# Layer 0's last four token tiles put among the first products of layer 1's convolution

## The chip, the cores and the metric

The kernel runs on one core of one Trainium2 chip. The metric is the device time of one execution in microseconds (us), the median of several runs. Engines are named as in the profile: PE is TensorE, DVE is VectorE, ACT is ScalarE, POOL is GpSimd, and SP issues nearly all DMAs. TensorE's loads of weights are shown as PEld.

## What is computed

Four transformer-like layers follow one another, each with an attention part and a feed-forward part, and each part ends in `x = layernorm(x + part(x))`. x has two samples of 1024 tokens and 1024 channels here. The change lies between the feed-forward part of layer 0 and the attention part of layer 1:

```python
# layer 0, feed-forward: a block-diagonal MLP on permuted channels
t = x[:, perm].reshape(tokens, 16, 64)
t = gelu(t @ up) @ down                  # per block, 64 -> 256 -> 64
x = layernorm(x + t.reshape(tokens, 1024)[:, argsort(perm)])
# layer 1, attention: first a convolution of width 3 along the tokens
y = conv1d(x, conv_w, "SAME") + conv_b   # 1024 -> 768 channels: q, k, v
# then attention in blocks of 128 tokens, 16 heads, and a projection
```

## The kernel before

The two samples are computed one after the other. Of a sample, `x` holds the eight tiles of 128 tokens (tokens on the partitions), and `xT` the same values turned (channels on the partitions, eight blocks k of 128 channels), with one zero column at either end for the convolution. Halves of 512 tokens are called th=0 (tiles 0 to 3) and th=1 (tiles 4 to 7).

**The end of layer 0** (`l0`). `blocks(th, extra)` runs the eight pairs of MLP blocks of one half: `ups` and `downs` on PE (L391, L409), `gelus` on ACT (L399), and a copy to `o` on DVE (L417) that POOL scatters by rows to `yd[th]` in DRAM by an indirect DMA (L418), which undoes the permutation. Each scatter waits for the one before it, since both write `yd[th]`. `back(th)` loads `yd[th]` again as eight pieces `y` of 128 channels by 512 tokens (L436, SP). For each tile `add_y` turns eight pieces of 128x128 on PE (L443) into two PSUM tiles, adds them to `x` on DVE (L131) and takes the statistics of the norm (`ln_stats`, L142 and L143); `ln_roots` makes the reciprocal roots (L150, ACT L156 and L157, DVE L159 to L162), `ln_scale` the norm itself (L165), and `to_xT` turns the tile on PE (L120) and copies it to `xT`, half on DVE (L97) and half on ACT (L99). The four tiles of th=0 are done inside `blocks(1)`. Those of th=1 come after it, tiles 4 and 5 with common roots, then tiles 6 and 7.

**The start of layer 1** (`l1_attn`). A pool opens with parameters and buffers (`qkv`, `qh`, `kh`, `u0`); it takes the place of `l0`'s pools, so its first writers wait until those are free. The convolution of width 3 makes two tokens at a time: four sums or differences of shifted columns of `xT` (j = 0 to 3), each multiplied by a weight of its own. For th=0 DVE writes these sums into `qh` (j = 0, 1) and `kh` (j = 2, 3), 256 columns for each of eight channel blocks (L546, eight operations of 128x1024); they see tokens -1 to 511 for j = 0, 1, 2, and to token 512 for j = 3. For th=1 POOL writes them in place into `xT` and `u0` (L546, 32 operations of 128x256). `conv(th, co)` is one of the six blocks of 128 output channels: it loads weights, multiplies 4 x 8 times (L579; each call shows as two matmuls of 256 columns in the trace, and j = 0, 1 share one PSUM tile, j = 2, 3 another), and puts the four together (`ce` on ACT L585, `cf` on DVE L589, `qkv` on DVE L592). This text calls the six blocks of th=0 c0 to c5. In sample 0 the two combined weights are made on DVE (L566 to L568, 128x1024 each) and stored to `cvd` in DRAM (L570), from where sample 1 and the second half load them.

In sample 0 c0 to c3 are followed by one step of `l2_dequant` each, which prepares a weight of layer 2: loads of scales and packed values (L1371, L1373), on DVE two unpackings (L1378, L1380) and two scalings (L1381), and two scatters to `wq` by POOL (L1382). All these weights share the pool `wp` with eight buffers of 512 KB, so a load waits until the last reader of a buffer is done. SP issues its DMAs in one order, and a DMA that waits holds all behind it.

**Who sets the order.** Inside `with self.tc.manual_schedule():` each engine gets its instructions in the order in which they are written. Outside, a scheduler orders them by priority when the program is built. Before, `l0`'s block is written by hand up to the norms of tiles 4 and 5; the tail with tiles 6 and 7 and the whole convolution of th=0 are left to the scheduler. What follows (heads, attention, the convolution of th=1) is by hand again and is not touched.

Of the kernel before, what the change touches and what calls it, by code (L numbers as in the profile page):

```python
# [8 lines left out]
F = mybir.dt.float32  # L9
# [8 lines left out]
P = 128  # L18
B = 2
S = 1024  # L20
D = 1024
NT = S // P
KD = D // P
HALF = 512
# [3 lines left out]
class Net:  # L28
# [96 lines left out]

    def add_row(self, row, tt):
        self.nc.gpsimd.tensor_tensor(self.x[:, tt, :], self.x[:, tt, :], row, ALU.add)

    def add_x(self, tt, half, p):
        xs = self.x[:, tt, half * HALF : (half + 1) * HALF]  # L130
# [62 lines left out]
    def l0(self, b):  # L193
        nc, i = self.nc, self.i
# [8 lines left out]
        with self.tc.tile_pool(name=self.nm("l0a"), bufs=1) as lp, self.tc.tile_pool(name=self.nm("l0b"), bufs=2) as tp:  # L203
# [27 lines left out]
            for th in range(2):  # L231
                for s, dst in ((0, qT), (1, kT), (2, v)):
                    p = self.ps()
# [202 lines left out]
                    nc.sync.dma_start(t, yd[th][k * P : (k + 1) * P, :])  # L436
                return ys

            def add_y(tt, ys):
                for g in range(2):  # L440
                    p = self.ps()
                    for j in range(4):
                        nc.tensor.transpose(  # L443
                            p[:, j * P : (j + 1) * P], ys[4 * g + j][:, (tt % 4) * P : (tt % 4 + 1) * P], self.ident
                        )
                    self.add_x(tt, g, p)
                self.ln_stats(tt)

            def line(th, first, n):


# [13 lines left out]
            with self.tc.manual_schedule():  # L465
                self.table()
                maxima(0)
                attend(0, {})
                maxima(1)
                e = line(0, project, (0, 1, 3, 4, 5, 6, 7, 8, 9))  # L470
                at(e, 9, lambda: store(0))
                at(e, 9, lambda: gather(0))
                attend(1, e)
                project(4)
                project(5)
                e = line(1, project, (-1, -1, 0, 0, 1, 1, 2, 2, 3))
# [7 lines left out]
                e = line(0, lambda tt: add_y(tt, ys), (2, 3, 3, 4, 5, 6, 6, 7, 7))  # L484
                blocks(1, e)
                ys = back(1)
                self.table()
                add_y(4, ys)
                add_y(5, ys)
                self.ln_roots([4, 5])  # L490
                for tt in (4, 5):
                    add_y(tt + 2, ys)
                    self.ln_scale(tt)
                    self.to_xT(tt)

        self.ln_roots([6, 7])
        for tt in (6, 7):
            self.ln_scale(tt)
            self.to_xT(tt)

    def l1_attn(self, b):
        nc, i = self.nc, self.i
        row = self.row("l1_projb")
        with self.tc.tile_pool(name=self.nm("l1a"), bufs=1) as lp, self.tc.tile_pool(name=self.nm("l1s"), bufs=2) as spool:
# [13 lines left out]
            nc.gpsimd.tensor_copy(identr, self.ident)  # L522
            bv = self.row("l1_bv")
            qkv = lp.tile([P, 6, S], F, name=self.nm("qkv"))

            qh = lp.tile([P, 8, HALF], F, name=self.nm("qh"))
            kh = lp.tile([P, 8, HALF], F, name=self.nm("kh"))
            u0 = lp.tile([P, HALF], F, name=self.nm("u0"))
# [29 lines left out]
            def conv(th, co):  # L558

                w = {}  # L560

                def load():
                    g = [self.w(i["l1_conv"][co, 0])]
                    if b == 0 and th == 0:
                        g1, g2, t = self.w(i["l1_conv"][co, 1]), self.w(i["l1_conv"][co, 2]), self.w()
                        nc.vector.tensor_tensor(t, g[0], g2, ALU.add)  # L566
                        nc.vector.tensor_tensor(t, t, g1, ALU.add)
                        nc.vector.scalar_tensor_tensor(g1, g1, -2.0, t, ALU.mult, ALU.add)  # L568
                        for n, f in enumerate((t, g1)):
                            nc.sync.dma_start(self.cvd[co, n], f)  # L570
                        w["w"] = [t, g1, g[0], g2]
                    else:
                        es = [self.w(self.cvd[co, n]) for n in range(2)]
                        w["w"] = es + g + [self.w(i["l1_conv"][co, 2])]

                def call(j, k):
                    if k == 0 and j % 2 == 0:
                        w["p", j // 2] = self.ps()
                    nc.tensor.matmul(  # L579
                        w["p", j // 2][:, 256 * (j % 2) : 256 * (j % 2) + 256], w["w"][j][:, k * P : (k + 1) * P],  # L580
                        moving(th, j, k), start=k == 0, stop=k == KD - 1,
                    )
                    if (j, k) == (2, 1):
                        w["e"] = spool.tile([P, 256], F, tag="ce", bufs=1, name=self.nm("ce"))
                        nc.scalar.activation(w["e"], w["p", 0][:, :256], AF.Identity, bias=cb2[:, co : co + 1])  # L585
                    if (j, k) == (2, 4):
                        w["f"] = spool.tile([P, HALF], F, tag="cf", bufs=1, name=self.nm("cf"))
                        for n, op in enumerate((ALU.add, ALU.subtract)):
                            nc.vector.tensor_tensor(w["f"][:, 256 * n : 256 * n + 256], w["e"], w["p", 0][:, 256:], op)  # L589

                def last():
                    nc.vector.scalar_tensor_tensor(  # L592
                        qkv[:, co, th * HALF : (th + 1) * HALF].rearrange("p (i s) -> p s i", s=2),
                        w["f"].rearrange("p (s i) -> p s i", s=2), 0.5,
                        w["p", 1].rearrange("p (s i) -> p s i", s=2), ALU.mult, ALU.add,
                    )

                return load, [lambda j=j, k=k: call(j, k) for j in range(4) for k in range(KD)], last

            first = conv(0, 0)  # L600
            first[0]()
            for j in range(4):
# [1196 lines left out]
```

## Time and profile before

| | us |
|---|---|
| median of 3 runs (5542.56 to 5547.45) | 5543.17 |
| the profiled execution, its own time | 5559.85 |
| its span in the profile | 5557.9 |
| PE busy in it | 5115.4 |
| DVE busy | 3199.0 |
| ACT busy | 1936.1 |
| POOL busy | 2021.7 |

The profile is of one execution, on the one core that is used; the granted TensorE clock was 0.948 of full speed over the span. Times in the prediction's steps are positions in this span. Sample 0 passes from layer 0 to layer 1 near 371 to 413 us, sample 1 near 3149 to 3185 us. In a line of the timeline the columns are start, duration, engine, line, operation, output and inputs, shapes and count; in brackets the idle time before it and what ended it. In a table by stage each engine's busy time stands in the order PE, PEld, DVE, ACT, POOL with its count of instructions.

### The profile page before, as it was taken

The numbers are of one execution on the slowest core, as the hardware profiler recorded it, in microseconds if no ns is written. First come the engines' busy times: TensorE is split into PE (matmuls) and PEld (weight loads), VectorE is DVE, ScalarE is ACT, GpSimd is POOL, SyncE is SP. The second block draws the span as 40 slices with busy tenths as digits, with TensorE's granted clock in tenths as the row PEclk, the third lists the DMA queues.
The fourth block names the chain that finished last, engine by engine and source line by source line (L and its number), as shares of the span: only waits on it lengthen the run. The fifth ranks groups of instructions, "written<-read, shape, count | busy, mean of one in ns | idle before, by whom it ended". The sixth has DMA issues, their size and how long they took to land.

```text
span 5557.9 us, 52406 instructions
## 1 busy us (share of the span) xinstructions
PE 5115.4 (92%) x17864; PEld 2586.7 (47%) x17864; DVE 3199.0 (58%) x4410; ACT 1936.1 (35%) x3925; POOL 2021.7 (36%) x1195
## 2 busy tenths in 40 slices
PE   9869989999999999998989799799999999999989
PEld 4436746444444444453444376464444444444533
DVE  3553245249999997214345412452599899953243
ACT  2230222257766542001013312222677665410110
POOL 1021220057778884100010211200677788831010
PEclk8789998999999999999988899989999999999999
DMA  2035310267787996110110333012777889951100
GB/s 92 33 131 174 103 43 33 100 182 221 210 234 222 259 258 197 61 60 13 55 63 33 115 123 103 32 44 87 212 215 204 243 219 264 264 177 45 61 8 30
DMA packets 263134, 725.28 MB, mean 130 GB/s; under 512 B 37425, under 2 KB 54449, under 8 KB 262869
## 3 DMA queue, kind: packets, MB, share of 16 engines
q1 hardware_dynamic: 256596, 700.97, 42.4%
q0 software_dynamic: 6272, 20.98, 1.1%
q8 instruction: 142, 2.33, 0.2%
q14 instruction: 124, 1.01, 0.1%
HBM read 616.70 MB, written 103.02 MB: 129 GB/s over the span
## 4 chain that ended last, share of the span: by engine, by line
PE 70%; DVE 14%; DMA 4%; ACT 3%; issue 2%; POOL 1%; SPq 0%; DVEq 0%; POOLq 0%; ACTq 0%
PE ps L104 28%; PE ps L1232 7%; PE ps L1122 6%; PE ps L579 5%; DVE h L1129 4%; PE ps L1151 4%; PE ps L1445 4%; PE ps L1271 3%; DVE h L1140 2%; PE ps L120 2%; PE ps L1185 2%; ACT ps L1124 1%; DVE x L165 1%; DVE st L142 1%; DMA w<-xcd 1%
## 5 line engine op out<-in xcount | busy, mean ns | idle before, releaser
L1114 POOL TENSOR_TENSOR h<-h,br 128x1024 f32<-128x1024 f32 x512 | 1204.3, 2374 | 27.6 <-DMA h<-dxd 20.0
L1124 ACT ACTIVATE ps<-ps,l_Alog 128x512 f32<-128x512 f32 x1024 | 668.8, 660 | 686.0 <-PE ps L1122 671.5
L1122 PE MATMUL ps<-hi,rep 128*128 128x512 f32 x1024 | 758.8, 741 | 22.9 <-DVE h L1129 14.6
L1129 DVE TENSOR_TENSOR_SCAN h<-ps,h 128x512 f32<-128x512 f32 x512 | 606.4, 1213 | 159.9 <-ACT ps L1124 159.8
L1129 DVE TENSOR_TENSOR_SCAN h<-ps,hst,h 128x512 f32<-128x512 f32 x512 | 643.8, 1304 | 11.7 <-ACT ps L1124 11.7
L1140 DVE TENSOR_TENSOR h<-h,ps 128x1024 f32<-128x1024 f32 x512 | 621.4, 1214 | 0.0
L104 PE MATMUL ps<-w,xT 128*128 128x512 f32 (+1 forms) x1280 | 518.3, 562 | 0.0
L1232 PE MATMUL ps<-xT,w 128*128 128x512 f32 x1024 | 511.0, 602 | 0.0
L1151 PE MATMUL ps<-h,sel 128*32 128x512 f32 x2048 | 404.5, 611 | 72.6 <-DVE h L1140 72.3
L1431 POOL TENSOR_TENSOR x<-x,row 128x1024 f32<-128x1024 f32 x48 | 112.9, 2353 | 883.4 <-PE ps L120 883.4
L131 DVE TENSOR_TENSOR x<-x,ps 128x512 f32<-128x512 f32 x192 | 129.9, 687 | 522.9 <-PE ps L104 372.5
L104 PE MATMUL ps<-xT,w 128*128 128x512 f32 x960 | 425.3, 599 | 0.2 <-DMA w<-l_wqkv 0.2
L1122 PE MATMUL ps<-lo,rep 128*128 128x512 f32 x1024 | 408.5, 399 | 0.0
L104 PEld LDWEIGHTS ps<-w,xT 128*128 128x128 f32 x1280 | 247.4, 195 | 255.3 <-issue 248.1
L1122 PEld LDWEIGHTS ps<-hi,rep 128*128 128x128 f32 x1024 | 196.0, 191 | 346.4 <-issue 242.1
L120 PE MATMUL ps<-ident,x 128*128 128x128 f32 x1024 | 168.5, 322 | 182.5 <-DVE x L165 155.8
L156 ACT ACTIVATE rs<-mv 128x1 f32<-128x1 f32 (+2 forms) x94 | 19.1, 203 | 786.4 <-DVE mv L150 786.2
L104 PEld LDWEIGHTS ps<-xT,w 128*128 128x128 f32 x960 | 183.8, 192 | 233.7 <-issue 230.4
L1122 PEld LDWEIGHTS ps<-lo,rep 128*128 128x128 f32 x1024 | 196.7, 192 | 201.0 <-issue 196.4
L1080 POOL TENSOR_TENSOR e<-e,one 128x512 f32<-128x512 f32 x64 | 81.5, 1273 | 563.5 <-ACT one L1077 381.0
L1271 PE MATMUL ps<-w,w 128*128 128x512 f32 x512 | 269.3, 608 | 0.0
L1185 PE MATMUL ps<-xT,w 128*128 128x512 f32 x512 | 266.1, 605 | 2.0 <-DVE h L1129 2.0
(268 smaller groups left out, 7579.6 us busy)
## 6 DMA issues: line engine op xcount, KB each, us to landing
h<-dxd SPq DMA_DIRECT2D x512, 512.0 KB
w<-l_in SPq DMA_DIRECT2D x128, 512.0 KB
w<-l_out SPq DMA_DIRECT2D x96, 512.0 KB
w<-l_conv SPq DMA_DIRECT2D x54, 512.0 KB
w<-cvd SPq DMA_DIRECT2D x36, 512.0 KB
w<-l_fw SPq DMA_DIRECT2D x32, 512.0 KB
xcd<-xo SPq DMA_DIRECT2D x64, 256.0 KB
szd<-zo SPq DMA_DIRECT2D x64, 256.0 KB
```

The source lines that it names most:

```text
L104: self.nc.tensor.matmul(out, lhsT, rhs, start=j == 0, stop=j == n - 1)
L120: nc.tensor.transpose(p[:, j * P : (j + 1) * P], self.x[:, tt, k * P : (k + 1) * P], self.ident)
L579: nc.tensor.matmul(w["p", j // 2][:, 256 * (j % 2) : 256 * (j % 2) + 256], w["w"][j][:, k * P : (k + 1) * P], moving(th, j, k), start=k == ...
L1114: nc.gpsimd.tensor_tensor(hs[k], hs[k], norms[of(k)[0]][1].unsqueeze(1).to_broadcast([P, 2, HALF]), ALU.mult)
L1122: nc.tensor.matmul(dA[k, m], rep[:, 8 * jj + 4 * m + q, :], hl[u, c][n], start=n == 0, stop=n == 1)
L1124: nc.scalar.activation(dA[k, m], dA[k, m], AF.Exp, scale=A[:, g : g + 1])
L1129: nc.vector.tensor_tensor_scan(hs[k][:, m, :], dA.pop((k, m)), hs[k][:, m, :], hst[:, g : g + 1] if u else 0.0, ALU.mult, ALU.add)
L1140: nc.vector.tensor_tensor(hs[k], hs[k], norms[of(k)[0]][3].unsqueeze(1).to_broadcast([P, 2, HALF]), ALU.mult)
L1151: nc.tensor.matmul(py[u, c][32 * j : 32 * j + 32, :], self.sel[:, q, :], hs[k - 1 + j // 2][:, j % 2, :], start=False, stop=q == 3,)
L1185: nc.tensor.matmul(p, w["w"][:, k * P : (k + 1) * P], self.xcols(k, u0, HALF), start=k == 0, stop=k == KD - 1)
L1232: nc.tensor.matmul(p, w["w"][:, k * P : (k + 1) * P], self.xcols(k, u * HALF, HALF), start=k == 0, stop=k == KD - 1)
L1271: nc.tensor.matmul(p, y[:, cc, t * P : (t + 1) * P], wt[:, cc * HALF : (cc + 1) * HALF], start=c2 == 0 and cc == 0, stop=last,)
```

## The change

`add_y` becomes a method of the class with the same body. `l0` ends with `blocks(1, e)` and returns `yd[1]`; the loads of `y` for th=1, and the additions, norms and transposes of tiles 4 to 7, move into `l1_attn`. There the pieces `y` are loaded into `vh`, a buffer of the heads that is empty at that time and is now made with the others. A block in written order holds c0 and c1 by j (eight calls each) with the four tiles between them: c0's j = 0, 1, 2 and c1's j = 0 come before tile 4, c0's j = 3 after tile 4 is turned. c1's `cf` is put into `u0`, so that c0's and c1's are alive together. The weights of c1 and then the pieces `y` are asked for before the first products. POOL's sums for th=1 are written after this block, and `l2_dequant(0)` to `(3)` follow c2 to c5 instead of c0 to c3. In the built order of each engine the instructions of everything after the heads stand as before.

```diff
@@ l0
-                ys = back(1)
-                self.table()
-                add_y(4, ys)
-                add_y(5, ys)
-                self.ln_roots([4, 5])
-                for tt in (4, 5):
-                    add_y(tt + 2, ys)
-                    self.ln_scale(tt)
-                    self.to_xT(tt)
-
-        self.ln_roots([6, 7])
-        for tt in (6, 7):
-            self.ln_scale(tt)
-            self.to_xT(tt)
+        return yd[1]
@@ l1_attn
+            vh = lp.tile([P, 4, D], F, name=self.nm("vh"))
...
                     if (j, k) == (2, 4):
-                        w["f"] = spool.tile([P, HALF], F, tag="cf", bufs=1, name=self.nm("cf"))
+                        if (th, co) == (0, 1):
+                            w["f"] = u0
+                        else:
+                            w["f"] = spool.tile([P, HALF], F, tag="cf", bufs=1, name=self.nm("cf"))
...
-            first = conv(0, 0)
-            first[0]()
-            for j in range(4):
+            def sums0(j):
                 for g in range(2):
                     ks = slice(4 * g, 4 * g + 4)
                     sums(nc.vector, 0, ks, [(j, (qh, kh)[j // 2][:, ks, 256 * (j % 2) : 256 * (j % 2) + 256])])
+            c0, c1 = conv(0, 0), conv(0, 1)
+            with self.tc.manual_schedule():
+                c0[0]()
+                sums0(0)
+                sums0(1)
+                c1[0]()
+                ys = [t for q in range(4) for t in (vh[:, q, :HALF], vh[:, q, HALF:])]
+                for k, t in enumerate(ys):
+                    nc.sync.dma_start(t, yd[k * P : (k + 1) * P, :])
+
+                def calls(c, j):
+                    for f in c[1][8 * j : 8 * j + 8]:
+                        f()
+
+                calls(c0, 0)
+                sums0(2)
+                calls(c0, 1)
+                calls(c0, 2)
+                calls(c1, 0)
+                self.table()
+                self.add_y(4, ys)
+                self.add_y(5, ys)
+                self.ln_roots([4, 5])
+                self.ln_scale(4)
+                self.add_y(6, ys)
+                self.to_xT(4)
+                self.ln_scale(5)
+                sums0(3)
+                calls(c1, 1)
+                self.to_xT(5)
+                calls(c0, 3)
+                c0[2]()
+                c2 = conv(0, 2)
+                c2[0]()
+                self.add_y(7, ys)
+                self.ln_roots([6, 7])
+                calls(c1, 2)
+                self.ln_scale(6)
+                self.to_xT(6)
+                self.ln_scale(7)
+                calls(c1, 3)
+                self.to_xT(7)
+                c1[2]()
             for k in range(KD):
                 sums(nc.gpsimd, 1, slice(k, k + 1), [(j, moving(1, j, k).unsqueeze(1)) for j in (2, 3, 0, 1)])
-            for co in range(6):
-                load, calls, last = conv(0, co) if co else first
-                if co:
+            for co in range(2, 6):
+                load, cs, last = conv(0, co) if co > 2 else c2
+                if co > 2:
                     load()
-                for f in calls:
+                for f in cs:
                     f()
                 last()
-                if b == 0 and co < 4:
-                    self.l2_dequant(co)
-
-            vh = lp.tile([P, 4, D], F, name=self.nm("vh"))
+                if b == 0:
+                    self.l2_dequant(co - 2)
@@ net_kernel
-            net.l0(b)
-            net.l1_attn(b)
+            net.l1_attn(b, net.l0(b))
```

More of the change, by code (lines that the diff above doesn't have):

```diff
@@ L127, in add_row, with add_y @@
         self.nc.gpsimd.tensor_tensor(self.x[:, tt, :], self.x[:, tt, :], row, ALU.add)
+    def add_y(self, tt, ys):
+        for g in range(2):
+            p = self.ps()
+            for j in range(4):
+                self.nc.tensor.transpose(
+                    p[:, j * P : (j + 1) * P], ys[4 * g + j][:, (tt % 4) * P : (tt % 4 + 1) * P], self.ident
+                )
+            self.add_x(tt, g, p)
+        self.ln_stats(tt)
     def add_x(self, tt, half, p):
@@ L437, in back @@
                 return ys
-            def add_y(tt, ys):
-                for g in range(2):
-                    p = self.ps()
-                    for j in range(4):
[L443 to L447, printed above, removed]
             def line(th, first, n):
@@ L483, in l0, with l1_attn @@
                 ys = back(0)
-                e = line(0, lambda tt: add_y(tt, ys), (2, 3, 3, 4, 5, 6, 6, 7, 7))
+                e = line(0, lambda tt: self.add_y(tt, ys), (2, 3, 3, 4, 5, 6, 6, 7, 7))
                 blocks(1, e)
-                ys = back(1)
-                self.table()
-                add_y(4, ys)
-                add_y(5, ys)
-                self.ln_roots([4, 5])
-                for tt in (4, 5):
-                    add_y(tt + 2, ys)
-                    self.ln_scale(tt)
-                    self.to_xT(tt)
-        self.ln_roots([6, 7])
-        for tt in (6, 7):
-            self.ln_scale(tt)
-            self.to_xT(tt)
-    def l1_attn(self, b):
+        return yd[1]
+    def l1_attn(self, b, yd):
         nc, i = self.nc, self.i
@@ L598, in conv @@
                 return load, [lambda j=j, k=k: call(j, k) for j in range(4) for k in range(KD)], last
-            first = conv(0, 0)
-            first[0]()
-            for j in range(4):
+            def sums0(j):
                 for g in range(2):
```

## The prediction

> **What bounds the kernel now.** I read the page first: TensorE (PE) is busy 92% of the span and holds 70% of the chain that ended last, so a change pays where PE stands still. Line 1 and the first line of part 4 of the page:
>
> ```profile
> PE 5115.4 (92%) x17864; PEld 2586.7 (47%) x17864; DVE 3199.0 (58%) x4410; ACT 1936.1 (35%) x3925; POOL 2021.7 (36%) x1195
> PE 70%; DVE 14%; DMA 4%; ACT 3%; issue 2%; POOL 1%; SPq 0%; DVEq 0%; POOLq 0%; ACTq 0%
> ```
>
> Then the table by stage: sample 0 from the last transposes of L0's blocks to the first product of the convolution, its first two output blocks (c0, c1), the pause before c2, c2 to c5; then sample 1: the same without a pause. Columns: stretch, length, busy us of each engine with counts, granted PE clock, DMA share, GB/s.
>
> ```profile
> 371.60:412.90 41.30, 15.59 (x65) 12.78 (x66) 28.27 (x49) 4.44 (x9) 1.29 (x4) 0.63 0.31 106
> 412.90:440.70 27.80, 27.78 (x130) 24.12 (x128) 16.80 (x12) 1.54 (x3) 20.93 (x34) 1.00 0.27 79
> 440.70:447.90 7.20, 0.01 (x1) 0.04 (x1) 2.57 (x3) 0.00 (x0) 0.24 (x1) 0.69 0.63 211
> 447.90:510.60 62.70, 58.85 (x256) 50.47 (x257) 24.21 (x30) 1.89 (x4) 5.85 (x4) 0.95 0.77 268
> 3149.20:3185.40 36.20, 15.59 (x65) 12.61 (x65) 24.81 (x47) 4.45 (x9) 1.29 (x4) 0.56 0.19 59
> 3185.40:3214.20 28.80, 28.80 (x130) 25.18 (x129) 3.96 (x8) 1.53 (x3) 19.15 (x32) 0.96 0.37 128
> ```
>
> The reader is to see 41.3 and 36.2 us in which PE works 15.6 us, at 0.6 of its clock: tiles 4 to 7 are fetched, added, normed and turned while nothing else is there for PE. One product block is 13.9 us when nothing holds it (27.8 for two). Last, the timeline around c0 in sample 0:
>
> ```profile
> 409.62 3.44 PE L120 MATMUL ps<-ident,x 128*128 128x128 f32 x16 [4.36 <-DVE x L165]
> 412.89 7.07 PE L579 MATMUL ps<-qh,w 128*128 128x256 f32 x32
> 413.57 1.22 DVE L546 TENSOR_TENSOR kh<-xT 128x1024 f32<-128x1024 f32 x1
> 413.75 1.52 POOL L546 TENSOR_TENSOR xT<-xT 128x256 f32<-128x256 f32 x1 [12.95 <-DVE xT L97]
> 416.92 15.98 POOL L546 TENSOR_TENSOR xT<-xT 128x256 f32<-128x256 f32 x28
> 423.61 9.84 DVE L1378 TENSOR_SCALAR w<-w 128x1024 int32<-128x1024 int32 x1 [2.30 <-DMA w<-l_packed]
> 434.62 0.68 DVE L592 SCALAR_TENSOR_TENSOR qkv<-cf,ps 128x512 f32<-128x512 f32 x1
> 445.26 1.23 DVE L566 TENSOR_TENSOR w<-w,w 128x1024 f32<-128x1024 f32 x1 [7.43 <-DMA w<-l_conv]
> 447.89 0.76 PE L579 MATMUL ps<-qh,w 128*128 128x256 f32 x1 [7.21 <-DVE w L567]
> ```
>
> L1378 usually takes 0.69 us; here it took 9.84 and ended when POOL's 32 sums (413.75 to 432.9, 19.2 us) did. That made c2's weights late and PE stood 7.2 us.
>
> **What the Trainium skill says.** "SBUF — State Buffer", section "Who interferes with whom": DVE and GpSimd share a port pair as an exclusive lock; a DVE instruction in a two-port mode, or with two SBUF inputs against a GpSimd reader, waits. The trace agrees: 9.84 for 0.69, and POOL's first sum took 1.52 for 0.60 beside L546. "TensorE: Matmul & The Clock Gate", "Part 1": PE runs at half clock until some 3.4 us of work. The trace agrees: after the 7.2 us pause 32 matmuls took 9.99 us, else 7.07; eight transposes take 1.94 or 1.09. "DMA: Bandwidth & Descriptors", "Queues, rings and completion order": each engine takes descriptors in ring order; here the cvd packets mostly flowed after those of the y loads issued before them.
>
> **The change, part by part.** No arithmetic is added or taken away; the order moves, twice (two samples). Durations are of the profiled execution (5559.85 us, span 5557.9), 16.7 us above the median 5543.17; I carry differences over.
>
> *The start of c0.* Its j=0, 1, 2 read no token beyond 511, so tiles 0 to 3 suffice. DVE, free at 371.8 (sample 1: 3149.5), makes sums of 1.2 us each; the little cb operation waits for its load, issued when L0's pool is free (last scatter landed, 3.4 us after issue as in sample 1, so 371.2). For that small load I estimate 2.2 us; it may be 1 to 4, which later waits hide. PE starts at about 373 (3151), cold. A j is 32 matmuls of 0.216 = 3.45 us. Sample 1: j=0 done 3156.5, j=1 3160, j=2 3163.4, c1's j=0 3166.9, transposes of tile 4, first full add at **3168.2**; y landed long before (issued about 3150.7, 9 us to land as before). Sample 0: c1's weight sums (3 of 1.25) stand before sums j=2, so PE has done c1's j=0 at 390.2. But SP issues the 8 y loads behind the four bias loads and the two cvd stores, which wait for those sums (381): issued from 381.5 (before: 376.2); 1 MB of stores, then 2 MB, at some 330 GB/s (before, 3.1 MB of both went from 377.5 to 387); last landing 392.5. First full add at **393.0** (386.17 before).
>
> *From that add (0).* Before, L162 ended 6.1 later; scale of tile 4 to 6.9. PE has paused 4.7: transposes cold 1.9, c1's j=1 3.45 plus 1 cold: 13.4. DVE meanwhile adds and norms tile 6 (2.6), copies, scales tile 5, makes sums j=3 (2.4): 13.4. Transposes 1.1, c0's j=3: 18.0. qkv of c0 18.8; in sample 0 c2's weights 3.8. Then tile 7: add 1.2, statistics 1.4, roots 1.4, cf 0.75, scale 0.8: 24.4 (28.1). Transposes, c1's j=3, transposes of tile 7: c2 starts at **30.5 (35.6)**.
>
> *Sample 1:* c2 at 3198.7 for 3214.2. What follows has no PE wait before and none after (weights of c2 to c5 are freed by PE as before): **15.5 us won**.
>
> *Sample 0:* c2 at 428.6 to 442.5, its weights long there. But dequantization 0 to 3 now goes with c2 to c5. POOL's sums start after tile 7's copy, at 429.0, and run 19.2 us to 448.2. The second dequantized half of step 0 (L1381, two SBUF inputs) comes just behind their start on DVE: by the lock it waits to 448.2. Behind it in DVE's queue are c3's weight sums; behind it on SP is c3's third load, whose buffer it frees: issued 449.5, landed 454 (before, the last of three took 5.5), two sums 2.5, c3 at 456.5. PE pauses 14.0. From there the kernel before has the pace with dequantization: c2 to c3 17.3, c3 to c4 17.15, then 13.9: end at 504.9 for 510.6: **5.7 won**. The scatter of that half, now behind the sums on POOL, lands at 454.6 (5.0, as 434.99 to 439.96); the idx load that waits for it on SP is reached later, at about 458. The two wq scatters and 3.8 us of DVE work that leave L0's end were costing the y loads 5 us there (376.2 for 371.2): in the 371.2 above. Loads for the heads stand behind dequantization 3 on SP, some 12 us into c5; wq is there before, wv is needed 27 us after. ACT's table load moves behind c1's j=0, hidden by the wait for tile 4.
>
> Sum: 15.5 + 5.7 = 21.2. 5543.2 - 21.2 = **5522**.
>
> Not seen before: a DVE operation with two SBUF inputs against a *row* of POOL sums. At 2789.46 one took 1.80 for 0.16 against one POOL operation. If it slips in between the sums it costs 0.6; if it waits for all, 19. I take 19.
>
> **The rivals.** *B, the lock does not hold.* For it: the DVE operation at 2789.46 got in between two POOL operations. Against: L1378 did not in 9.84 us. Then c3 starts at 442.5; the next dequantization still waits for the scatter behind POOL's sums (453.2), 3.9 of DVE work, a load and sums 7.0: c4 at 464.2, cold 15.4, c5 13.9: 493.5, 17.1 won, in all 32.6: 5510.5. *C, PE stays cold* (slower): the pauses put among the products keep the clock at half through c0 and c1, 27.7 us more, some 5 counted already. Sample 1 loses 23 - 15.5 = 7.5. In sample 0 the wait for y hides part; 19.5 - 5.7 = 14 lost: 5564.7. It decides from about 10.6 us of cold time more per sample. For it: clock 0.56 to 0.63 in this stage. Against: c0 ran at 7.07 straight after cold transposes, and after a pause of 3.1 (482.37) at 7.14. *D, given back:* y in sample 0 lands 5 late and each of the three pauses costs 1.5 more: some 5 and 5 us, 5532 to 5537, within the noise.
>
> **How the numbers follow.** A 0.60, B 0.22, D 0.12, C 0.06. About 0.2% (11 us) is what a measurement can tell: faster below 5532. A is spread by about 7 us (landing of y, c3's load, cold clock), so one part in twenty of A and B falls short: faster 0.79, same 0.15, slower 0.06. Range 5505 to 5538: from B's fast side to D's end; C and the rest, 2 in 10, left out.
>
> **What would show it.** In the table by stage c2 starts 15 (sample 1) and 19 us (sample 0) earlier. In sample 0 an L1381 operation or a weight sum of up to 19 us stands beside POOL's sums, and PE waits some 14 us for DVE's weights before c3. y loads are issued at 381 or so in sample 0. It is wrong if c3 follows c2 at once (B), if products among the transposes take over 5 us a j (C), or if PE waits for y past 395 (D).

## The result and the profile after

The kernel after takes **5515.69 us** (median of 5 runs, 5507.26 to 5520.49) against 5543.17 us for the kernel before on the same chip: 27.5 us or 0.5% less, ratio 0.995, 95% interval 0.9935 to 0.9964. The forecast was 5522, range 5505 to 5538, and faster by over 0.2%. The profiled execution took 5520.49 us (span 5518.8). Line 1 of its page:

```profile
PE 5101.6 (92%) x17864; PEld 2585.1 (47%) x17864; DVE 3193.2 (58%) x4410; ACT 1935.9 (35%) x3925; POOL 2022.9 (37%) x1195
```

PE's busy time is 13.8 us less for the same 17864 matmuls, in spans that differ by 39.1. Of these 13.8, 5.6 lie in the stage of the two samples, which ran at a higher granted clock (0.91 and 0.94 from the last transposes of L0's blocks to the heads, 0.85 and 0.86 before); the rest lies in parts that both kernels have alike. The table by stage of the kernel after, with the columns of the one before: sample 0 from the last transposes of L0's blocks to c2, c2 and c3, the pause before c4, c4 and c5; then sample 1 up to c2, and c2 and c3.

```profile
361.98:417.52 55.54, 41.44 (x200) 35.72 (x201) 38.78 (x62) 5.29 (x11) 2.29 (x5) 0.88 0.37 133
417.52:445.30 27.78, 27.78 (x130) 24.16 (x128) 9.57 (x13) 1.53 (x3) 23.15 (x33) 1.00 0.43 152
445.30:454.50 9.20, 0.01 (x1) 0.00 (x0) 5.40 (x7) 0.00 (x0) 2.38 (x2) 0.68 0.71 232
454.50:488.00 33.50, 30.11 (x129) 25.91 (x130) 14.57 (x18) 0.95 (x2) 3.82 (x4) 0.93 0.79 267
3127.12:3178.63 51.51, 41.73 (x200) 36.15 (x201) 29.77 (x53) 5.29 (x11) 1.29 (x4) 0.87 0.34 113
3178.63:3206.26 27.63, 27.63 (x130) 24.36 (x129) 3.25 (x7) 1.54 (x3) 18.25 (x32) 1.00 0.47 152
```

The stretch with the transposes now holds c0 and c1 as well: 41 us of PE work in 51 to 56 us, at 0.87 to 0.88 of the clock, where before 15.6 us of work stood in 36 to 41 us and c0 and c1 followed. In sample 0 the pause of 7.2 us before c2 is gone, and one of 9.2 us stands before c4 and one of 3.4 before c5.

A position in one profile is not comparable with the same in another: the stage of sample 0 starts 8.5 us later in the profile of before, behind a part that both kernels have alike. So I measure from the end of the last product of L0's MLP in each sample (366.67 and 3144.38 before, 358.19 and 3123.33 after). In us from there, "after" with a second profile from another chip:

| | c0 | c2 | c3 | c4 | c5 | heads |
|---|---|---|---|---|---|---|
| sample 0 before | 46.22 | 81.22 | 98.55 | 115.70 | 130.08 | 143.97 |
| sample 0 after | 6.82 | 59.34 | 73.15 | 96.35 | 115.92 | 129.81 |
| sample 0 after, again | 6.83 | 59.65 | 73.46 | 96.65 | 115.06 | 128.95 |
| sample 1 before | 41.05 | 69.83 | 83.64 | 97.45 | 111.26 | 125.08 |
| sample 1 after | 7.07 | 55.31 | 69.12 | 82.94 | 96.75 | 110.56 |
| sample 1 after, again | 6.71 | 52.91 | 66.73 | 80.54 | 94.36 | 108.17 |

The stage is 14.2 (15.0) us shorter in sample 0 and 14.5 (16.9) in sample 1, together 28.7 us in the first profile: the 27.5 of the medians. The prediction had 5.7 and 15.5. Sample 0 is where it went differently. PE's own timeline of the kernel after there:

```profile
365.01 7.14 PE L567 MATMUL ps<-qh,w 128*128 128x256 f32 x32 [1.97 <-issue]
...
380.14 3.10 PE L134 MATMUL ps<-ident,vh 128*128 128x128 f32 x24
388.70 1.94 PE L120 MATMUL ps<-ident,x 128*128 128x128 f32 x8 [5.47 <-DVE x L176]
390.44 5.42 PE L567 MATMUL ps<-qh,w 128*128 128x256 f32 x16
...
410.11 1.97 PE L120 MATMUL ps<-ident,x 128*128 128x128 f32 x8 [5.60 <-DVE x L176]
411.87 4.94 PE L567 MATMUL ps<-kh,w 128*128 128x256 f32 x16
...
431.34 7.07 PE L567 MATMUL ps<-qh,w 128*128 128x256 f32 x32
...
454.54 9.31 PE L567 MATMUL ps<-qh,w 128*128 128x256 f32 x32 [9.22 <-DVE w L555]
...
474.11 7.14 PE L567 MATMUL ps<-qh,w 128*128 128x256 f32 x32 [3.35 <-DVE w L555]
```

L567 is the product of the convolution in the new file, L134 `add_y`, L120 `to_xT`, L176 the norm. In sample 0 PE stands twice, 5.5 us each, for the norm of a tile, and the product behind (16 matmuls) takes about 5 us where 3.62 is warm. c3 at 431.34 has no bracket: it follows c2 at once, so the pause of 14 us that the forecast put there didn't come. The pause stands before c4 instead. The timeline of all engines in that stretch (L1412 and L1414 the unpackings, L1415 the scaling, L1416 the scatter, L554 to L556 c3's and c4's weight sums):

```profile
416.85 0.69 DVE L1414 TENSOR_SCALAR w<-w 128x1024 int32<-128x1024 int32 x1 [3.04 <-PE ps L567]
418.24 3.30 POOL L534 TENSOR_TENSOR xT<-xT 128x256 f32<-128x256 f32 x4 [3.16 <-DVE xT L97]
418.65 1.27 DVE L1415 SCALAR_TENSOR_TENSOR w<-w,w 128x1024 f32<-128x1024 int32 x1
...
422.62 17.78 POOL L534 TENSOR_TENSOR xT<-xT 128x256 f32<-128x256 f32 x26
423.95 1.50 DVE L554 TENSOR_TENSOR w<-w,w 128x1024 f32<-128x1024 f32 x1 [4.03 <-DMA w<-l_conv]
...
440.56 0.98 POOL L1416 DMA_INDIRECT wq<-w,idx  x1 [0.16 <-issue]
443.94 0.33 SPq L1402 DMA_DIRECT2D idx<-l_perm  x1
443.95 0.69 DVE L1412 TENSOR_SCALAR w<-w 128x1024 int32<-128x1024 int32 x1 [11.72 <-DMA wq<-w,idx]
444.38 3.48 SPq L80 DMA_DIRECT2D w<-l_conv  x3
```

The scaling L1415 has two SBUF inputs and comes 0.4 us behind the start of POOL's sums. It took 1.27 us, not 19, and L554, which has two SBUF inputs as well, took 1.50 in the middle of the row instead of 1.22. POOL's sums pay as well: 22.2 us in all instead of 19.2. Behind them on POOL stands the scatter (440.56); SP's idx load waits for it to 443.94, and c4's three weight loads stand behind that on SP.

### The profile page after: what moved, and what is told of

It reads as the page before. It is cut to its first block, busy times and chain, and to the rows that moved or that the text cites. A ratio compares the mean times of both kernels' runs of the same rounds, so it can differ in the third digit from the quotient of the medians.

```text
span 5518.8 us, 52401 instructions
## 1 busy us (share of the span) xinstructions
PE 5101.6 (92%) x17864; PEld 2585.1 (47%) x17864; DVE 3193.2 (58%) x4410; ACT 1935.9 (35%) x3925; POOL 2022.9 (37%) x1195
## 4 chain that ended last, share of the span: by engine, by line
PE 51%; DVE 10%; DMA 3%; ACT 2%; issue 1%; POOL 1%; SPq 0%; DVEq 0%; POOLq 0%; ACTq 0%
PE ps L104 22%; PE ps L1479 4%; PE ps L1156 4%; PE ps L1266 3%; PE ps L567 3%; DVE h L1163 3%; PE ps L1185 3%; PE ps L1305 3%; PE ps L120 2%; DVE h L1174 1%; DVE x L176 1%; PE ps L1219 1%; ACT ps L1158 1%; PE ps L271 1%; PE ps L305 1%
## 5 line engine op out<-in xcount | busy, mean ns | idle before, releaser
L1148 POOL TENSOR_TENSOR h<-h,br 128x1024 f32<-128x1024 f32 x512 | 1204.7, 2375 | 32.6 <-DMA h<-dxd 28.7
L120 PE MATMUL ps<-ident,x 128*128 128x128 f32 x1024 | 161.7, 312 | 174.1 <-DVE x L176 154.7
L104 PEld LDWEIGHTS ps<-xT,w 128*128 128x128 f32 x960 | 184.1, 192 | 233.0 <-issue 231.2
L1266 PEld LDWEIGHTS ps<-xT,w 128*128 128x128 f32 x1024 | 188.3, 191 | 172.8 <-issue 148.9
```

Of the source, the lines that this page charges most:

```text
L104: self.nc.tensor.matmul(out, lhsT, rhs, start=j == 0, stop=j == n - 1)
L120: nc.tensor.transpose(p[:, j * P : (j + 1) * P], self.x[:, tt, k * P : (k + 1) * P], self.ident)
L1148: nc.gpsimd.tensor_tensor(hs[k], hs[k], norms[of(k)[0]][1].unsqueeze(1).to_broadcast([P, 2, HALF]), ALU.mult)
L1266: nc.tensor.matmul(p, w["w"][:, k * P : (k + 1) * P], self.xcols(k, u * HALF, HALF), start=k == 0, stop=k == KD - 1)
```

## The experiments

**One sample at a time.** Theory: both samples gain about the same. In each of two kernels one sample keeps the order before.

```diff
+WOVEN = (1,)
...
+                if not (b in WOVEN):
+                    ys = back(1)
...
+            if b in WOVEN:
+                c0, c1 = conv(0, 0), conv(0, 1)
...
+            else:
+                first = conv(0, 0)
+                first[0]()
```

This is the first of the two; the second has `(0,)`. The branches hold the new order and the order before.

> The new order is used for sample 1 alone; sample 0 keeps the order before, instruction by instruction on each engine. Theory 1 (the two samples gain about the same, 13.6 in sample 1 and 14 to 15 in sample 0, as the two profiles say once the 8 to 9 us that the profile of before lost ahead of the changed stage are taken out): 13 to 15 us faster than before, 5528 to 5530. The prediction's split (15.5 in sample 1, 5.7 in sample 0): 15.5, about 5527.5 (then sample 0 would hold only 12 of the 27.5). Rival (sample 0 holds most of the gain, and what is won in sample 1 is given back later): under 8 us, above 5535.

Measured: ratio 0.9968 (0.9958 to 0.9978), 17.8 us (12 to 23) of 5554.05 on that chip. In the profile the stage of sample 1 is 110.51 us long (125.08 before), that of sample 0 144.05 (143.97 before).

> The new order is used for sample 0 alone; sample 1 keeps the order before, instruction by instruction on each engine. Theory 1 (sample 0 gains about as much as sample 1, since c3 follows c2 without a wait): the heads of sample 0 come 14 to 16 us earlier against the start of that sample's stage, those of sample 1 no more than that; total 12 to 17 us under the kernel before on the same chip. The prediction's split: 5.7 us. Rival (the gain of sample 0 in the profile after came from that execution, not from the order): 0 to 4 us.

Measured: ratio 0.9976 (0.9966 to 0.9986), 13.3 us (8 to 19) of 5546.99. The stage of sample 0 is 128.95 long, that of sample 1 124.78. So each sample's gain comes from its own weave, 15.0 us in sample 0 and 14.6 in sample 1. Both lie inside the intervals of the times, so no loss later in the kernel shows. The 8.5 us ahead of the stage are no gain of the change: L0's last product of sample 0 ends at 366.67 in the one profile of before and at 352 to 361 in all the others, with nothing changed ahead of it, and 28.7 and 8.5 together are more than the interval of the times allows (20 to 36 us).

**What a row of POOL sums keeps out.** The prediction's main step rested on this, so I put operations beside the row that touch nothing else: on `vh`, which is empty then.

```diff
                 c1[2]()
+                if b == 0:
+                    nc.vector.tensor_tensor(vh[:, 2, :], vh[:, 1, :], vh[:, 3, :], ALU.add)
+                    nc.vector.tensor_scalar(vh[:, 0, :], vh[:, 1, :], 1.0, None, ALU.mult)
```

> Two operations are added on DVE in sample 0, right behind c1's qkv and so just behind the start of POOL's 32 sums (418.2 to 440.4 in the profile after): first vh2 = vh1 + vh3 (two SBUF inputs, 128x1024, 1.2 us alone), then a copy of vh1 to vh0 by tensor_scalar (one SBUF input, 128x1024, 0.69 us alone, the kind that took 9.84 us in the kernel before). vh holds nothing at that time and is written again later. Theory 1 (the exclusive port lock keeps out only the two-port kind behind a row of POOL operations; operations with two SBUF inputs slip in between): the addition takes 1.3 to 1.6 us, the copy some 17 to 20 us and ends with the last sum, at about 440; c3's weight sums stand behind it, so c3 starts at about 448 instead of 431.3, and the end of the stage (heads) comes 8 to 10 us later than after. Theory 2 (the prediction's step: a two-SBUF-input operation is locked out as well): the addition itself takes some 20 us. Theory 3 (no lock by a row of sums; the 9.84 us of before were a single event): 1.5 and 0.7 to 1.0 us, nothing moves.

Measured: the addition took 1.27 us and the copy behind it 1.10; c3 started 13.8 us after c2 as in the kernel after. The addition refutes the prediction's step, and the copy my theory 1, which kept it out. But the unpackings of the kernel before (9.84 us) and of the kernel with the old order in sample 0 (9.52) had ended with the row. The next probe asked whether integer operations differ. It put a bitwise `tensor_scalar` on int32 in the place of the copy.

> Probes for what kind of DVE operation a row of POOL sums keeps out. In the runs so far an unpacking (tensor_scalar on int32) took 9.84, 9.52, 3.60 and 18.81 us and each time ended with the row, while a float tensor_scalar of the same size right behind an addition took 1.10 us. In sample 0, behind c1's qkv: an addition of two halves of vh (float, 128x1024), then a bitwise tensor_scalar on int32 from vh to vh. In sample 1, behind c2's qkv, some 4 to 5 us before the row ends: a float tensor_scalar (times 1.0), then an addition. vh holds nothing at these times and is written again later. Theory K (the kind decides: the integer form needs the lock, the float form does not): in sample 0 the integer operation takes 15 to 18 us and ends with the row, and heads come about 10 us late as after the fill; in sample 1 the float one takes 0.7 to 1.1 us. Theory T (the moment decides: an operation that directly follows one that has already slipped in gets its turn, one that comes to the row on its own is kept out): in sample 0 the integer operation takes 0.7 to 1.1 us; in sample 1 the float one waits for the row's end, 3 to 5 us.

Measured: 1.10 us for the integer form too. Theory K falls. The two operations meant for sample 1 were placed ahead of the row when the program was ordered, so that half tells nothing. The last probe took the addition away, and tied the operation of sample 1 to c2's result, so that it must come in the middle of the row:

```diff
+                if b == 0:
+                    nc.vector.tensor_scalar(
+                        vh[:, 0, :].bitcast(I), vh[:, 1, :].bitcast(I), 15, None, ALU.bitwise_and
+                    )
...
                 last()
                 if b == 0:
                     self.l2_dequant(co - 2)
+                elif co in (2, 4):
+                    nc.vector.tensor_scalar(vh[:, 0, :HALF], qkv[:, co, :HALF], 1.0, None, ALU.mult)
```

> In the two earlier probes an operation with one SBUF input, float or integer, took 1.10 us (1.02 until the next one began) although POOL's row of sums was running, but it stood directly behind an addition with two SBUF inputs. Here in sample 0 the integer tensor_scalar on vh (128x1024) stands alone behind c1's qkv, without the addition; in sample 1 a float tensor_scalar (128x512, from qkv to vh) stands behind c2's qkv, in the last 4 to 5 us of the row of sums, and the same one again behind c4's qkv, where no row is, as its price alone. vh holds nothing at these times. Theory T (an operation that comes on its own while the row runs is kept out until the row ends; it gets in only behind one that has already slipped in between): sample 0 some 17 to 19 us for the integer operation, c3 late by 13 to 16 us as with the fill; sample 1 some 4 us against 0.3 to 0.6 alone. Theory S (only the start of the row matters: what comes when POOL's first sum has just begun gets in): 0.7 to 1.1 us in sample 0 and some 4 us in sample 1. Theory N (neither is kept out; the waits of 3.6 to 18.8 us have another cause in the dequantization): under 1.2 us in both.

Its timeline, first in sample 0, then in sample 1 (L643 and L658 are the probes):

```profile
412.49 3.74 POOL L534 TENSOR_TENSOR xT<-xT 128x256 f32<-128x256 f32 x4 [3.04 <-DVE xT L97]
412.90 0.74 DVE L643 TENSOR_SCALAR vh<-vh 128x1024 int32<-128x1024 int32 x1
...
3177.17 14.84 POOL L534 TENSOR_TENSOR xT<-xT 128x256 f32<-128x256 f32 x26
3187.96 4.33 DVE L658 TENSOR_SCALAR vh<-qkv 128x512 f32<-128x512 f32 x1
3215.58 0.43 DVE L658 TENSOR_SCALAR vh<-qkv 128x512 f32<-128x512 f32 x1
```

In the middle of the row the float operation took 4.33 us and ended at 3192.29, 0.3 us after the row (3177.17 + 14.84 = 3192.01); without a row it takes 0.43. In sample 0, 0.4 us behind the first sum's start, the integer one took 0.74. That is what theory S said. So for a copy-like operation with one SBUF input neither the type nor an addition ahead of it decides: near the start it can get in, and in the middle it waits for the whole row, not for one sum. But the place is not the only thing that differs. L643 began while DVE was still ending the operation ahead of it, and so did the two of 1.10 us; L658 and the unpackings of 9.84, 9.52 and 3.60 us came to a DVE that stood idle, if only for 0.03 us. Whether an operation that DVE already has in hand gets in at any place of the row is a rival that no run tries.

An operation with two SBUF inputs gets in at the start and in the middle alike, also from idle (L554 above, 4.03 us): those of this size took 1.27 to 1.63 us beside the row, for 1.22. What it waits for seems to be the one POOL operation that it meets. Beside a long one the price is higher, as two lines of the last experiment's timeline (the dequantizations moved) show; there L127 is an addition on POOL, the second of the two from 777.98 to 780.85, and L1418 a scaling of 1.22 us:

```profile
775.29 5.57 POOL L127 TENSOR_TENSOR x<-x,row 128x1024 f32<-128x1024 f32 x2 [2.96 <-PE ps L120]
778.68 3.25 DVE L1418 SCALAR_TENSOR_TENSOR w<-w,w 128x1024 f32<-128x1024 int32 x1
```

**Filling PE's two pauses.**

```diff
                 self.add_y(6, ys)
+                calls(c1, 1)
                 self.to_xT(4)
                 self.ln_scale(5)
                 sums0(3)
-                calls(c1, 1)
...
                 self.ln_scale(6)
+                calls(c1, 3)
                 self.to_xT(6)
                 self.ln_scale(7)
-                calls(c1, 3)
```

> c1's products j=1 are put ahead of the transposes of tile 4, c1's j=3 ahead of the transposes of tile 6; the products need nothing of these tiles. Theory 1 (the weave loses time where PE stands for the norm of a tile, 5.5 and 5.6 us in each sample, and runs cold behind it): a product of 3.45 us fills each of the two pauses, and some of the 1.5 to 2 us lost on cold products is won; DVE's chain to tile 7 is little changed, so c2 starts 2 to 5 us earlier in each sample, 4 to 10 in all; total 5506 to 5512. Rival (DVE's chain of additions, norms and copies for tiles 4 to 7 sets c2's start, PE's order does not): c2 starts within 1 us of before the edit, since each transposition waits for DVE all the same; total within 2 us of 5515.7.

Measured: ratio 0.9957 (0.9942 to 0.9972), no gain over the kernel after. But c2 of sample 0 starts at 55.21 in the stage (59.34 after): the fill won 4.1 us there, and in sample 1 it is 50.92 (52.91 in the profile of after with as warm a start, so 2.0). The two pauses of 5.5 and 5.6 us that I had put down to each sample are those of sample 0; in sample 1 the second is 1.94 us (before 3171.69), so there is less to fill. What took it back in sample 0 is in the timeline of all engines:

```profile
416.63 18.81 DVE L1414 TENSOR_SCALAR w<-w 128x1024 int32<-128x1024 int32 x1
416.66 0.62 POOL L534 TENSOR_TENSOR xT<-xT 128x256 f32<-128x256 f32 x1
...
418.93 15.96 POOL L534 TENSOR_TENSOR xT<-xT 128x256 f32<-128x256 f32 x28
...
435.47 2.06 SPq L80 DMA_DIRECT2D w<-l_conv  x3
...
447.75 0.77 PE L567 MATMUL ps<-qh,w 128*128 128x256 f32 x1 [17.18 <-DVE w L555]
```

The second unpacking of dequantization 0, which in the kernel after ended 0.7 us before the first sum (417.54 and 418.24), now meets it and waits 18.81 us, to the end of the row. c3's loads on SP wait for the buffer that it frees (435.47), and PE stands 17.2 us before c3. This is the chain that the prediction laid out, set off by another operation than it named. Why this one was kept out at the very start of the row, where L643 above was not, the runs don't say. By the traces it began 0.03 us ahead of the first sum, L643 0.41 behind it, and both while DVE was ending the operation ahead of them.

**The sums later on POOL.** The statement of the sums is moved behind the loop over c2 to c5.

```diff
-            for k in range(KD):
-                sums(nc.gpsimd, 1, slice(k, k + 1), ...)
             for co in range(2, 6):
                 ...
+            for k in range(KD):
+                sums(nc.gpsimd, 1, slice(k, k + 1), ...)
```

> POOL's 32 sums for th=1 are written behind c2 to c5 in the code. In the built order of POOL in sample 0 the second scatter of dequantization 0 then stands behind 9 sums instead of 32; 23 sums follow it, ahead of dequantization 1's scatters. Theory 1 (the 9.2 us that PE waits before c4 come from that scatter standing behind the sums: it lets SP go on with the idx load, behind which c4's weight loads stand): the idx load is issued at about 430 instead of 443.9, c4's wait falls from 9.2 to 0 to 3 us, its cold start (9.3 for 7.1 us) mostly goes, and the stage of sample 0 ends 6 to 11 us earlier; total about 5505 to 5510 against 5515.7. Some of it may come back at c5, if dequantization 1's scatters behind the 23 sums now hold dequantization 2. Rival (c4's weights wait for a buffer or for the memory, not for the scatter): c4's wait stays at 7 to 9 us, total within 3 us of 5515.7. Sample 1 has no scatter there and must not move.

Measured: ratio 0.9934 (0.9919 to 0.995). In its timeline of all engines (here L1413 is the unpacking, L1403 the idx load):

```profile
424.02 1.97 POOL L1417 DMA_INDIRECT wq<-w,idx  x1 [0.16 <-issue]
426.01 14.35 POOL L534 TENSOR_TENSOR xT<-xT 128x256 f32<-128x256 f32 x23
428.40 0.33 SPq L1403 DMA_DIRECT2D idx<-l_perm  x1
...
437.31 3.60 DVE L1413 TENSOR_SCALAR w<-w 128x1024 int32<-128x1024 int32 x1 [5.59 <-DMA w<-l_packed]
...
451.46 0.77 PE L567 MATMUL ps<-qh,w 128*128 128x256 f32 x1 [6.66 <-DVE w L555]
```

The scatter comes out between the sums, and the idx load at 428.40 instead of 443.94, as theory 1 had it. But c4's wait fell only from 9.2 to 6.7: the next unpacking is caught by the rest of the row (3.60 for 0.69), after 5.6 us in which DVE waited for its packed weights. Stage of sample 0: 126.62, 2 to 3 us won, too little to show in the time (0.995 and 0.9952 for the kernel after). The scatter was one of the two ways in which the row held c4; an unpacking kept out by the row is the other.

**No row at all in sample 0.** There DVE makes the 32 sums, eight behind each block in the code.

```diff
-            for k in range(KD):
-                sums(nc.gpsimd, 1, slice(k, k + 1), ...)
...
+                eng = nc.gpsimd if b else nc.vector
+                for k in (2 * co - 4, 2 * co - 3):
+                    sums(eng, 1, slice(k, k + 1), ...)
```

> The kernel after with one edit: in sample 0 the 32 sums for th=1 are made by DVE, spread between c2 and c3, not by POOL; no fill. Theory 1 (the row on POOL costs sample 0 the wait before c4, through the scatter behind it): c2 starts as in the kernel after, c3 follows at once, the wait before c4 falls from 9.2 to 0 to 4 us; the stage of sample 0 ends 5 to 10 us earlier; sample 1 does not move; total 5 to 10 us under the kernel after, 0.993 to 0.9945 of before. Rival (the 15 us of the version with both edits come from the fill alone): c4's wait stays, total within 3 us of the kernel after (0.995).

Measured: 5508.13 us, ratio 0.9921 (0.9903 to 0.9939); the kernel after had 0.9939 to 0.9964 on another chip, so by the time alone the two intervals just touch. PE in its timeline:

```profile
443.09 8.83 PE L567 MATMUL ps<-qh,w 128*128 128x256 f32 x32 [2.91 <-DVE w L555]
...
458.83 7.14 PE L567 MATMUL ps<-qh,w 128*128 128x256 f32 x32
```

c4's wait is 2.91, c5's gone; no unpacking takes over 0.7 us. The stage of sample 0 is 120.28 us long, 9 less than after, and that of sample 1 (111.38) is not shorter. The row of sums on POOL was most of what held sample 0's later blocks.

**Both together**, the fill and DVE's sums:

> c1's products j=1 and j=3 ahead of the transposes of tiles 4 and 6 as in the fill, and in sample 0 the 32 sums for th=1 are made by DVE, spread between c2 and c3, so that no row of sums stands on POOL. Theory 1 (what is left in sample 0 is the row of sums: it keeps out the unpackings and holds the scatter that SP's idx load waits for): no unpacking takes over 1.5 us, c2 starts about 4 us earlier as in the fill, c3 follows it at once, c4's wait is 0 to 5 us instead of 9.2; the stage of sample 0 ends 8 to 15 us earlier than after, sample 1 2 to 4; total 10 to 18 us under the kernel after on the same chip. Rival (the chain of c4 and c5 is the memory: packed weights, stores and loads of some 7 us each): the waits come back as 'DMA' waits of 5 to 9 us at c4 and c5, and the total is 4 to 8 under after, the part of the fill alone. A loss is possible if the 32 sums, 11 to 12 us of DVE work, delay c3's weights.

Measured: 5504.42 us against 5519.32 for the kernel after on the same chip, ratio to before 0.9923 (0.9906 to 0.9941) against 0.9952 (0.9939 to 0.9964): 15 us better by the medians, though the intervals still meet at their ends. c2 starts at 55.58 in the stage of sample 0, c3 and c4 follow without a wait, but c5 now waits 4.2 us for its weights and runs cold (10.07 for 7.07), so that the stage ends at 118.81, only 1.5 us before that with DVE's sums alone. The two versions can't be told apart by the time. What the fill wins at c2, the loads of c5 take back: there theory 1's rival is right.

> The kernel after once more, unchanged, so that the other runs are compared with it on one chip. From the first comparison: 0.9935 to 0.9964 of the kernel before, 20 to 36 us. In sample 0 c3 follows c2 without a wait and c4 waits some 9 us, as in the first profile; if c3 waits 10 us or more here, the order of the second unpacking and the start of POOL's sums is a race that falls either way from run to run.

The kernel after, measured again, stands as before: 0.9952, c3 without a wait, 9.2 us before c4.

**The dequantizations out of the way.** From the last version, the four steps are put among the scores of the second half of the attention.

```diff
-                if b == 0:
-                    self.l2_dequant(co - 2)
...
-                attend(line(0, wp), 2)
+                calls = line(0, wp)
+                if b == 0:
+                    for c in range(4):
+                        calls.insert(5 * c + 4, lambda c=c: self.l2_dequant(c))
+                attend(calls, 2)
```

> The version with the fill and DVE's sums, and the four dequantizations of sample 0 taken out of c2 to c5 and put among the scores of the second half of the attention, where few weights are loaded. Theory 1 (what is left of the waits in c2 to c5 is the dequantization's loads, scatters and buffers): c2 to c5 of sample 0 follow one another without a wait, 55.3 us, so the heads come about 8 us earlier than in the version with the fill and DVE's sums (476.1 in its profile); in the attention it costs PE 0 to 6 us; total 2 to 8 us under that version, 0.990 to 0.992 of the kernel before. Rival (it only moves: scatters on POOL between the weights of the scores, and loads ahead of those that the feed-forward part needs, cost as much there): total within 3 us of that version, or slower.

Measured: 5526.88 us, ratio 0.9954 (0.9937 to 0.9971): some 17 us worse than the version it starts from, by the two ratios. The stage itself did what theory 1 says, 112.84 us with c2 to c5 without a wait. Most of the loss is in the attention. Its PE waits between 600 and 800 us, then POOL in the timeline there (L1419 the scatter, L723 the weights of the scores):

```profile
PE ps L730 <- POOL s L723: 31.7, 7, 10.8
```

```profile
734.53 1.20 POOL L1419 DMA_INDIRECT wq<-w,idx  x1 [7.17 <-DVE w L1418]
...
740.82 0.96 POOL L1419 DMA_INDIRECT wq<-w,idx  x1 [5.09 <-DMA wq<-w,idx]
741.80 2.04 POOL L723 TENSOR_TENSOR s<-s,l1r 128x512 f32<-128x512 f32 x2
742.91 1.12 PE L730 MATMUL ps<-ident,s 128*128 128x128 f32 x4 [10.75 <-POOL s L723]
```

POOL's second scatter waits 5 us for the first to land, and the weights of the scores stand behind it; PE waits 31.7 us for POOL there, where the version with both edits has 9.6 (the profile is of the slowest of the six executions, 5544.2 us). The rival is right.

## Why the prediction was right, and where not

**The start of c0** was right: 6.3 and 6.6 us after L0's last product were forecast, 6.8 and 7.1 came. ("A j is 32 matmuls" is a slip: it is 16 in the trace, and 16 of 0.216 us make the 3.45.) The cold start was overrated in sample 0 (7.14 for the 32 matmuls, where 7.07 is warm) and came in sample 1 (8.83).

**The landing of y in sample 0** was put too late. SP's own timeline there, in the kernel after:

```profile
370.70 1.59 SPq L558 DMA_DIRECT2D cvd<-w  x2
372.34 4.17 SPq L607 DMA_DIRECT2D vh<-yd  x8
```

SP issued the loads 14.2 us into the stage (14.8 forecast), behind the two cvd stores as said. But PE found y there for tile 4 at 22.0 (380.14), without a wait; the forecast had 25.8. The rate was as forecast, 330 GB/s from 370.70 to 380.20. What was wrong is the start: the forecast let all 3 MB flow after the loads' issue, while the stores were on their way from 12.5 us on. So the first full add came at 23.3 instead of 26.3 in the stage, and of these 3.0 us 2.6 were left when c2 started (59.3 for 61.9).

**From that add to c2**, 35.6 and 30.5 us were forecast; it took 36.0 and 31.4. The chain of additions, norms and transposes was right in its order; PE's pauses were 5.5 instead of 4.7 us, and the cold products cost 1.3 to 1.8 us instead of 1. Two of the four groups of 16 among the transposes took over 5 us (5.42 and 5.21), which the forecast had named as a sign of rival C. C still did not come: the other groups ran at 3.6 to 3.7, and the cold time added to the products is 3 us in sample 0 and 5 in sample 1, where C needed 10.6 more in each.

**Sample 1**: 15.5 us forecast, 14.5 and 16.9 measured in two profiles, 17.8 (12 to 23) by the time of the kernel with that part alone. Of the 2.4 us between the two profiles 1.7 are the clock at c0: 8.83 against 7.14 us.

**Sample 0**: 5.7 us forecast, 14.2 and 15.0 measured. The step that failed is "I take 19", for an operation with two SBUF inputs beside a row of POOL sums: it costs 0.3. With it the pause of 14 us before c3 fell away, and rival B's chain took over: c4 was forecast there at 97.5 in the stage and came at 96.35, held by the scatter behind POOL's sums. B's own end, 126.8, was 2 to 3 us too early, since c5 waits 2.2 to 3.4 us for its weights, which B left out. That c3 follows c2 at once is the sign that the text had named for B. It had given both prices of that operation, 0.6 and 19, and took the larger; it had the trace's one case (1.80 us, between two POOL operations) on the other side, and that case was the better witness.

**What was read into the lock.** The Trainium skill, "SBUF — State Buffer", section "Who interferes with whom", says of a DVE instruction in a two-port mode and GpSimd that whoever issues first holds the shared pair "for the whole instruction" and that the other fully blocks; of two SBUF inputs it says only that they contend with a GpSimd reader. For one instruction against one, this case agrees with it: beside the probe L643 a POOL sum took 1.05 us for 0.60, beside the scaling L1415 1.59. I had stretched it to a row. For a one-input operation in the middle of the row that stretch is what the runs show (9.84, 9.52, 3.60 and 4.33 us, to the row's end each time, and 18.81 from its start with the fill); for a two-input operation it is not (1.50 for 1.22). That the waits come from this lock is the page's reading; the runs show only who waited and how long.

**The total.** 5522 was forecast and 5515.7 measured. That this lies within the spread given to A, the main forecast, is luck: A's mechanism did not occur in sample 0, whose surprise was 9 us where B had 11.4. B's own total, 5510.5, is as near. It had been right to leave C out (the clock in the stage is 0.87, not 0.6); by its mechanism B should have had more than 0.22.

## What to carry to other kernels

Work that waits on a chain of other engines gains PE's time only as far as independent products can be put into its pauses, and the gain shows where the next supply (here weights, scatters and a queue of loads) is late. Where a row of GpSimd operations runs beside DVE, look for DVE operations with one SBUF input and an SBUF output (here `tensor_scalar`) that would come in the middle of it: one of 0.7 us can stand for the whole row, and an order that is faster elsewhere can push it there. Before an asynchronous scatter goes to GpSimd, look at what stands in front of it there and who waits for it.

## What was not expected of the hardware

- A row of 32 GpSimd operations, one every 0.57 us, keeps a DVE `tensor_scalar` with one SBUF input out to the end of the row (4.33 for 0.43 us, 18.81 for 0.69), although the row has 31 seams; an operation with two SBUF inputs gets in at a seam. Near the start of the row three of the one-input kind got in (0.74, 1.10, 1.10 us). What decides at the start is open.
- How long PE paused does not tell whether the next products run cold. In sample 1 it seems to: the first 32 products of c0 took 8.83 to 9.78 us in each of the five profiles with a pause of 2.21 to 2.26 us before them, and 7.14 to 7.30 in each of the six with one of 1.81 to 1.85. But in sample 0 the pause before c0 was 1.96 to 1.98 us in eleven profiles, and the same 32 took 7.14 or 7.15 us in eight of them and 8.83, 9.88 and 9.93 in the other three. Behind whole blocks without a gap a pause of 3.35 us (before c5, kernel after) left them at 7.14, and one of 2.91 (before c4, with DVE's sums) did not: 8.83. This was only observed, not tried.
